# Sixth output pair and one tile of the seventh transposed on VectorE, the last tile on TensorE, rows of output pairs loaded two products sooner

## The chip, the core and the metric

The kernel runs on one core of a Trainium2 chip. The core has TensorE (PE in the profile; its weight loads are PEld), VectorE (DVE), ScalarE (ACT), GpSimd (POOL) and SyncE (SP). DMAs are issued from the queues of SP, ACT and POOL. The metric is the device time of one execution in microseconds; less is better. All data are fp32.

## What is computed

The reference, cut to what matters:

```python
def reference(x, adj, W_q, b_q, W_k, b_k, W_v, b_v):
    h = jnp.maximum(_layernorm(x, axis=-1), 0.0)            # x: 2708 x 1024
    q, k, v = h @ W_q.T + b_q, h @ W_k.T + b_k, h @ W_v.T + b_v
    z = (q @ k.T) / sqrt(1024) * adj                        # adj: 2708 x 2708, about 4 ones in a row
    z = jnp.where(z == 0.0, -10000.0, z)
    return x + jax.nn.relu(softmax(z, axis=1) @ v)
```

## The kernel before

**Algebra.** W_q and W_k are multiplied first, so that a query row is one product of h with a matrix M, and a score is the dot product of a query row with a gathered row of h. The softmax-weighted sum of gathered rows of h gives a tile u of 128 rows and 1024 columns, and u times W_v is the output before relu and the addition of x. Rows are sorted by their number of ones in adj, so that a tile needs as many gathers as its fullest row has ones. There are 22 tiles.

**Units.** TensorE works through 20 units, numbered from 0. Units 0 to 9 are query pairs. Units 10 to 19 are output pairs, of the tiles (6, 5), (4, 3), (2, 0), (20, 7), (17, 13), (18, 12), (19, 11), (15, 10), (14, 1) and (16, 9); the sixth output pair is thus unit 15, the seventh unit 16. Tile 8 stands alone behind them and is called the single tile. A pair is done by seven products of blocks instead of eight (`multiply`, L1045): `s2`, `a12`, `s4`, `s3` of the unit, then `a11` and `s1` of the next one (`opened`), then `a22` of the unit. Every product is four matmuls of 128x512 in the program (eight rows of the trace, since fp32 takes two passes), all in `add_block`, L1011. Between the products the function `after(i)`, i from 0 to 6, does the work of other engines for slot i.

**Turning.** A product needs its left operand transposed. There are two ways. TensorE turns a tile with eight 128x128 matmuls against an identity (`half_turned`, L415; the results `pt` lie in PSUM; ScalarE copies them out as `a11`, `a12`, `a22`, L718, or VectorE reads them in the sums `s1` and `s3`, L722). Or the tile is "faced": when its sum u is complete, ScalarE writes a permuted copy v (L945), v goes to `u_dram`, SP loads it in four quarters (`by_quarters`, L700), and VectorE transposes 32x32 blocks, two instructions of 128x512 per tile (`faces`, L705). The function `sums` decides which way a tile goes when it is complete (L940). A tile that is not faced is stored and loaded whole (L951, L1212), or, if its unit is near, kept in SBUF as `u` (`held`).

**Attention.** VectorE forms the scores (L863, one instruction per gathered 128x1024 block), the weights (L906 to L911), and the sums u (L923, one instruction per gathered block; the first block of a tile is scaled by ScalarE, L912). These steps are a generator that `after` advances by a fixed number of estimated microseconds per slot, less a little for faced tiles. The gathered blocks `g` are loaded by indirect DMAs that POOL issues (L610) into slots that VectorE's sums set free; query tiles `pq` come by SP (L833). L929 is the last sum of the single tile, half a tile high.

**Order.** VectorE's instructions stand in program order from unit 4 on; TensorE's, ScalarE's, POOL's and SP's are placed by the scheduler when the program is built. Each engine then runs its own list in order and waits on semaphores. Rows of output pairs (`or`) are loaded by `load_rows` in slot 4 two units ahead (slot 2 in units 4 and 9). Seven buffers hold rows, sums and permuted copies.

Of the kernel before, what the change touches and what calls it, by code (L numbers as in the profile page):

```python
# [10 lines left out]
FT = mybir.dt.float32  # L11
# [7 lines left out]
P = 128  # L19
# [46 lines left out]
def tile_preln_masked_attention(  # L66
# [13 lines left out]
    N, D = x.shape  # L80
    DC = D // P
# [336 lines left out]
    def turned(xt, name):  # L418

        hT = work.tile([P, D], FT, tag="hT", name=f"T_{name}", bufs=2).rearrange("p (c q) -> p c q", q=P)  # L420
        for s in range(DC // 4):
            nc.scalar.copy(hT[:, s * 4:(s + 1) * 4, :], half_turned(xt, s))
        return hT
# [190 lines left out]
    rows_of = {}  # L614
# [88 lines left out]
    def faces(dst, xt, lo, hi):  # L703

        return nc.vector.transpose(dst.rearrange("p c (g r) -> p g c r", r=QP),  # L705
                                   xt.rearrange("p (g c r) -> p g c r", g=QUADS, r=QP)[:, :, lo:hi])
# [212 lines left out]
    def sums(t):  # L919
        u, coef, m = us.pop(t)  # L920
        for s in range(0 if t in EMPTY else 1, K[t]):
            fill()
            chained(lambda: nc.vector.scalar_tensor_tensor(  # L923
                u, g_of[t][s], coef[:, s:s + 1], u, op0=ALU.mult, op1=ALU.add))
            free.append(g_of[t][s])
            yield 1.3
        fill()
        if t in HOSTS:
            chained(lambda: nc.vector.scalar_tensor_tensor(  # L929
                u[:HP], g_of[t][K[t]][:HP], m[:HP, 3:4], u[:HP], op0=ALU.mult, op1=ALU.add))  # L930
            free.append(g_of[t][K[t]])
            yield 1.3
            fill()
        g_of.pop(t)
        if t == SECOND:
            nc.sync.dma_start(v_dram, u)
            whole_second.append(True)
            return
        unit = next((n for n, pair in enumerate(units) if pair[0] == "o" and t in pair[1:]), len(units))
        if now < [unit - 2, 2] and unit <= len(q_pairs) + 4 or unit >= len(units) - 1:  # L940
            faced_tiles.add(t)
        print("done", t, "at", now, "unit", unit, t in faced_tiles)
        if t in faced_tiles:
            v = row_tile(f"v_{t}")
            nc.scalar.copy(v.rearrange("p (a c r) -> p c a r", a=QUADS, r=QP),  # L945
                           u.rearrange("p (c a r) -> p c a r", a=QUADS, r=QP))
            nc.scalar.dma_start(u_dram[t * P:(t + 1) * P, :], v)
        elif near(t):
            held[t] = u
        else:  # L950
            nc.sync.dma_start(u_dram[t * P:(t + 1) * P, :], u)  # L951
        done.add(t)
# [277 lines left out]
    for n, unit in enumerate(units):  # L1230
        kind, ta, tb = unit
        now[:] = n, 0
        if n == FIRST:
            ordered.close()
            ordered.enter_context(tc.manual_schedule(engines={mybir.EngineType.DVE}))
            nc.sync.dma_start(bp_dram, bp_sb[0:1, :])
        turn = n in (0, FIRST - 1)
        share = (20.9 if n < len(units) - 5 else 21.5) / 7
        nxt = units[n + 1] if n + 1 < len(units) else None
        if nxt is not None and nxt[0] == "o":  # L1240
            share -= 2.3 / 7 * len(set(nxt[1:]) & faced_tiles)
        results = (q_results if kind == "q" else o_results)(ta, tb)

        def after(i):
            now[1] = i
            add_due()
            if (n, i) in steps_ahead:
                follow(steps_ahead[n, i])
            if (n, i) == (2, 5):
                owe(8)  # L1250
                owe(9)
                rows_of[FIRST] = load_rows(units[FIRST])
                owe(10)
                owe(6)
                owe(7)
                rows_of[FIRST + 1] = load_rows(units[FIRST + 1])
                pooled.close()
            if n == FIRST and i in (1, 4, 5):
                for g in slots[:4] if i == 1 else slots[4:6] if i == 4 else slots[6:8]:
                    with tc.issue_after(sorted_at[-1].ins):  # L1260
                        nc.vector.memset(g, 0.0)
            b11, b12, b21, b22 = M[:, 0, 0], M[:, 0, 1], M[:, 1, 0], M[:, 1, 1]
            for at, place, src in (((-1, 0), b12, of_wv(0, 1)), ((0, 0), b11, of_wv(0, 0)), ((0, 2), T[:, 1], of_wv(1, 1)),
                                   ((0, 3), b21, of_wv(1, 0)), ((0, 4), b22, of_wv(1, 1))):
                if (n - last_q, i) == at:
                    nc.sync.dma_start(place, src)
            for at, place, a, b in (((0, 2), T[:, 0], b12, b11), ((0, 4), T[:, 1], T[:, 1], T[:, 0]),
                                    ((1, 0), T[:, 2], b22, b12), ((1, 1), T[:, 3], b21, T[:, 1])):
                if (n - last_q, i) == at:
                    nc.vector.tensor_sub(place, a, b)  # L1270
            if (n - last_q, i) == (1, 1):
                free.extend(M.rearrange("p i j (a c) w -> p i j a (c w)", a=2)[:, 0, 1, a, :] for a in range(2))
            if (n, i) == (FIRST, 5):
                next(stream)
            if (n, i) == (FIRST, 6):
                chain.append(behind[-1])
                next(stream)
                nc.vector.tensor_tensor(bad, bad, total, op=ALU.not_equal)
            if (n, i) == (FIRST + 1, 6):
                marked(EARLY, NT)  # L1280
            if (n, i) == (FIRST + 2, 4):
                nc.vector.tensor_scalar(msq, msq, MLIMIT, None, op0=ALU.is_gt)
            if n > FIRST + 1 or n == FIRST + 1 and i > 1:
                advance(share)
            if nxt is not None:

                if i == (3 if n == 0 else 4 if turn else 0):
                    ops_of[n + 1] = blocks(*rows_of[n + 1], nc.gpsimd if n + 1 < FIRST - 1 else None)
                    with tc.issue_after(products[-1].ins) if n + 1 == FIRST else nullcontext():
                        ops_of[n + 1][1]()  # L1290
                if i == (4 if n == 0 else 5 if turn else 2):
                    ops_of[n + 1][2]()
                    rows_of.pop(n + 1)
                    if n == last_q - 1:
                        all_rows()
                if i == 3:
                    banks_of[n + 1] = banks_for(bp_sb)
                if i == 6 and n + 2 < FIRST:
                    natural_rows(n + 2)
                if i == (2 if n in (FIRST, last_q) else 4) and n + 2 > FIRST and n + 2 < len(units) and n + 2 not in rows_of:  # L1300
                    while units[n + 2][0] == "o" and not done.issuperset(units[n + 2][1:]):
                        advance(1.0)
                    rows_of[n + 2] = load_rows(units[n + 2])
            if (n, i) in steps_at:
                follow(steps_at[n, i])
            if (n, i) == (3, 4):
                searched()
            if (n, i) == (3, 6):
                for s in range(8, HIGH):
                    for c in range(0, D, D // 4):  # L1310
                        with tc.issue_after(entered[-1].ins):
                            nc.gpsimd.memset(slots[s][:, c:c + D // 4], 0.0)
            if i == 3 and units[n - 1][0] == "o" and NT - 2 in units[n - 1][1:]:
                tail(NT - 1)
            if nxt is None and i == 1:
                uT = work.tile([P, D], FT, tag="hT", name="T_alone", bufs=2).rearrange("p (c q) -> p c q", q=P)
                faces(uT, single["rows"], 0, DC)
                single["turned"] = uT
            if n == len(units) - 2 and i == 6:
                while alone not in done:  # L1320
                    advance(1.0)
                single["rows"], = load_rows(("o", alone))
            if nxt is None and i == 3:
                single["banks"] = banks_for(bp_sb)
            if n == last_q - 1 and i == 4:

                nc.sync.dma_start(bp_sb, bv.to_broadcast([P, D]))
            if (n, i) == (last_q, 1):
                nc.vector.tensor_sub(bp_sb[:, NB:], bp_sb[:, NB:], bp_sb[:, :NB])

        multiply(n, results, after)
# [231 lines left out]
```

## Time and profile before

| what | us |
|---|---|
| median of 3 runs (lowest, highest) | 637.94 (637.57, 638.15) |
| the profiled execution | 638.0 |
| its span, from first to last instruction | 636.3 |
| TensorE busy in the span | 624.6 |
| VectorE busy | 525.7 |
| ScalarE busy | 283.5 |
| GpSimd busy | 361.8 |
| mean granted clock of TensorE | 0.995 |

In timelines the first number of a row is the start in us from the beginning of the span, the second the time until the last of the merged instructions ends, xN their count, and brackets hold the idle time of the engine before the row and who ended it. In the chain of waits the first number is the time, the second how long the chain stayed there.

### The profile page before, as it was taken

What the parts mean: (1) busy time and instruction counts of PE and PEld (TensorE: products, weight loads), DVE (VectorE), ACT (ScalarE), POOL (GpSimd) and SP (SyncE); (2) the same over time, 40 slices, a digit from 0 to 9 for tenths busy, and PEclk for the clock granted to TensorE, in tenths of its full rate; (3) what the DMA queues carried; (4) which work ended last, traced back from release to release, by engine and by line L of the source; (5) the groups of instructions that cost most, each with busy time, mean ns of one, the idle gap of its engine ahead of it and who ended that gap; (6) DMA issues with size and microseconds to landing.
All of it is one profiled execution on the core that took longest, in us unless ns stands there. A gap on an engine that the chain in (4) does not pass through costs nothing.

```text
span 636.3 us, 6139 instructions
## 1 busy us (share of the span) xinstructions
PE 624.6 (98%) x1627; PEld 315.5 (50%) x1627; DVE 525.7 (83%) x1021; ACT 283.5 (45%) x421; POOL 361.8 (57%) x383
## 2 busy tenths in 40 slices
PE   9999999999999999999999999999999999999994
PEld 5777766444444544444444434444444444444441
DVE  5999889897995755997889999999999989898341
ACT  3539975859667533424341243443343333422300
POOL 2649960975868277563742563576566777632431
PEclk9999999999999999999999999999999999999997
DMA  8998897598696439986699998999999999893761
GB/s 339 407 372 310 334 351 298 199 342 328 246 382 221 170 113 334 326 299 196 194 289 323 297 412 216 311 318 324 351 378 321 334 299 295 242 289 95 210 217 40
DMA packets 62352, 180.11 MB, mean 283 GB/s; under 512 B 10039, under 2 KB 17031, under 8 KB 61672
## 3 DMA queue, kind: packets, MB, share of 16 engines
q0 software_dynamic: 25136, 78.41, 39.4%
q1 hardware_dynamic: 31242, 80.19, 35.8%
q10 hardware_dynamic: 5934, 21.06, 8.5%
q8 instruction: 15, 0.25, 0.2%
q14 instruction: 25, 0.20, 0.1%
HBM read 147.23 MB, written 42.31 MB: 298 GB/s over the span
## 4 chain that ended last, share of the span: by engine, by line
PE 85%; DVE 6%; issue 4%; DMA 3%; SPq 1%; POOL 0%; ACT 0%; POOLq 0%; DVEq 0%; ACTq 0%
PE ps L1011 38%; PE psy L1011 28%; PE ps_y L476 6%; PE ps_x L476 4%; PE ps_z L476 4%; PE pt L415 3%; DVE u L923 2%; DMA g<-h_dram,tab 1%; DMA or<-u_dram 1%; DVE junk L863 1%; DVE s L722 1%; DVE wlow L1270 1%; PE ps_y L511 1%; SPq L700 1%; DVE q L1092 0%
## 5 line engine op out<-in xcount | busy, mean ns | idle before, releaser
L610 POOL DMA_INDIRECT g<-h_dram,tab x94 | 121.4, 1291 | 84.4 <-DVE u L923 31.1
L1011 PE MATMUL ps<-M,a 128*128 128x512 f32 x320 | 144.0, 593 | 0.0
L1011 PE MATMUL psy<-wlow,s 128*128 128x512 f32 x320 | 143.9, 592 | 0.0
L863 DVE SCALAR_TENSOR_TENSOR junk<-g,pq 128x1024 uint8<-128x1024 f32 x93 | 113.7, 1222 | 14.0 <-DMA g<-h_dram,tab 10.9
L1011 PEld LDWEIGHTS ps<-M,a 128*128 128x128 f32 x320 | 59.8, 190 | 70.8 <-issue 70.6
L1011 PEld LDWEIGHTS psy<-wlow,s 128*128 128x128 f32 x320 | 59.7, 190 | 70.2 <-issue 69.4
L923 DVE SCALAR_TENSOR_TENSOR u<-g,coef,u 128x1024 f32<-128x1024 f32 x69 | 88.4, 1281 | 6.9 <-ACT u L912 5.8
L389 DVE FIND_INDEX8 at<-ones,adj 128x8 uint32<-128x685 f32 (+1 forms) x88 | 74.5, 865 | 0.0
L1011 PE MATMUL psy<-wlow,a 128*128 128x512 f32 x160 | 72.0, 593 | 1.4 <-DVE q L1092 1.4
L1011 PE MATMUL ps<-M,s 128*128 128x512 f32 x160 | 72.1, 592 | 0.0
L1011 PE MATMUL ps<-wlow,s 128*128 128x512 f32 x160 | 72.0, 593 | 0.1
L368 ACT ACTIVATE sized<-adj 128x2708 uint8<-128x2708 f32 (+1 forms) x22 | 54.3, 2468 | 7.5 <-DMA adj<-in_adj_dram 6.2
L298 POOL TENSOR_TENSOR hsum<-hsum,x 128x256 f32<-128x256 f32 (+1 forms) x56 | 38.7, 729 | 25.6 <-DVE wlow L444 21.2
L1110 POOL DMA_INDIRECT y<-in_x_dram,tab x19 | 34.8, 1832 | 29.1 <-ACT y L1127 15.9
L1011 PEld LDWEIGHTS psy<-wlow,a 128*128 128x128 f32 x160 | 30.3, 190 | 40.0 <-issue 37.1
L1011 PEld LDWEIGHTS ps<-wlow,s 128*128 128x128 f32 x160 | 30.3, 190 | 38.6 <-issue 37.9
L1011 PEld LDWEIGHTS ps<-M,s 128*128 128x128 f32 x160 | 30.3, 190 | 38.1 <-issue 37.4
L912 ACT ACTIVATE u<-g,coef 128x1024 f32<-128x1024 f32 x18 | 20.7, 1147 | 32.1 <-DVE coef L911 32.1
L808 POOL DMA_INDIRECT out_dram<-y,tab x21 | 25.0, 1188 | 16.4 <-DVE flag L1354 6.1
L626 POOL DMA_INDIRECT tab_dram<-tab,pos_i x22 | 21.9, 995 | 20.7 <-DVE pos_i L689 15.3
L276 ACT ACTIVATE x<-x,r 128x1024 f32<-128x1024 f32 (+1 forms) x22 | 25.9, 1235 | 7.3 <-POOL r L266 7.3
L760 ACT COPY ps<-bp_sb 128x512 f32<-128x512 f32 x42 | 24.5, 595 | 7.2 <-DVE y L1145 6.7
(251 smaller groups left out, 843.5 us busy)
## 6 DMA issues: line engine op xcount, KB each, us to landing
adj<-in_adj_dram SPq DMA_DIRECT2D x21, 1354.0 KB, 11.3
x<-in_x_dram SPq DMA_DIRECT2D x21, 512.0 KB, 3.9
h_dram<-x ACTq DMA_DIRECT2D x21, 512.0 KB, 8.7
u_dram<-v ACTq DMA_DIRECT2D x13, 512.0 KB, 6.4
or<-u_dram SPq DMA_DIRECT2D x52, 128.0 KB, 7.0
q_late<-q SPq DMA_DIRECT2D x12, 512.0 KB, 6.0
pq<-q_late SPq DMA_DIRECT2D x12, 512.0 KB, 8.6
M<-in_wv_dram SPq DMA_DIRECT2D x4, 1024.0 KB
```

What stands on the lines that cost most here:

```text
L276: nc.scalar.activation(xs[i][:n], xs[i][:n], AF.Relu, bias=r[:n, 4, i:i + 1], scale=r[:n, 3, i:i + 1])
L298: small.append(nc.gpsimd.tensor_add(hsum[:n, cols], hsum[:n, cols], xt[:n, cols]))
L368: nc.scalar.activation(sized[:n], a[:n, :, :PW], AF.Abs, accum_out=total[:n, t:t + 1])
L389: nc.vector.max_index(at[:n, k - first_k, g, :], ones[:n, 0:8], a[:n, g, :])
L476: mm = nc.tensor.matmul(bank, a_tile(o + H * a[0], a[1], i), b(o), start=first and o == 0, stop=(o == H - 1), skip_group_check=True)
L610: return nc.gpsimd.indirect_dma_start(out=dst, out_offset=None, in_=src, in_offset=off, bounds_check=N - 1, oob_is_err=False)
L760: nc.scalar.copy(return_[h], row[:, h * NB:(h + 1) * NB])
L808: to = nc.gpsimd.indirect_dma_start(out=out, out_offset=bass.IndirectOffsetOnAxis(ap=ptab.bitcast(U32)[:n, t, SLOTS:SLOTS + 1], axis=0), i ...
L863: chained(lambda: nc.vector.scalar_tensor_tensor(junk, g_of[t][s], 1.0, tq[t], op0=ALU.mult, op1=ALU.mult, accum_out=zall[:, t, s:s + 1]))
L923: chained(lambda: nc.vector.scalar_tensor_tensor(u, g_of[t][s], coef[:, s:s + 1], u, op0=ALU.mult, op1=ALU.add))
L1011: mm = nc.tensor.matmul(bank, a[:, c, :], b[:, c, :], start=False, stop=(c == 3), skip_group_check=True)
L1110: return nc.gpsimd.indirect_dma_start(out=y[:n], out_offset=None, in_=x, in_offset=off, compute_op=ALU.add)
```

## The change

It has three parts. Tiles up to unit 16 may be faced, if they are complete by slot 0 two units ahead (before: up to unit 14, by slot 1). The single tile is no longer faced: it stays in SBUF, and TensorE turns it in slot 1 of the last unit. And rows of an output pair are loaded in slot 2 instead of 4 when both tiles are complete by then.

```diff
@@ sums
-        if now < [unit - 2, 2] and unit <= len(q_pairs) + 4 or unit >= len(units) - 1:
+        if now < [unit - 2, 1] and unit <= len(q_pairs) + 6 or unit == len(units) - 1:
             faced_tiles.add(t)
@@ after
-                if i == (2 if n in (FIRST, last_q) else 4) and n + 2 > FIRST and n + 2 < len(units) and n + 2 not in rows_of:
+                ready = n >= last_q and n + 2 < len(units) and done.issuperset(units[n + 2][1:])
+                if (i == 4 or i == 2 and (n == FIRST or ready)) and n + 2 > FIRST and n + 2 < len(units) and n + 2 not in rows_of:
                     while units[n + 2][0] == "o" and not done.issuperset(units[n + 2][1:]):
                         advance(1.0)
                     rows_of[n + 2] = load_rows(units[n + 2])
@@ after
             if nxt is None and i == 1:
-                uT = work.tile([P, D], FT, tag="hT", name="T_alone", bufs=2).rearrange("p (c q) -> p c q", q=P)
-                faces(uT, single["rows"], 0, DC)
-                single["turned"] = uT
-            if n == len(units) - 2 and i == 6:
                 while alone not in done:
                     advance(1.0)
-                single["rows"], = load_rows(("o", alone))
+                r, = load_rows(("o", alone))
+                single["turned"] = turned(r, "alone")
```

`turned` (L420) is the kernel's own function for one whole tile: two calls of `half_turned` and two copies by ScalarE (L422). In the changed program tiles 18, 12 and 19 are faced beside those that were before; tile 11, the other one of unit 16, is not.

The first place is TensorE's list where tile 18 was turned, at the seam of units 13 and 14. In the names `or_18` is the loaded tile 18, `u_11` a tile in SBUF, and the last number counts buffers. Before:

```order
L1011 MATMUL psy_2825<-wlow_171,a22_2740 128x512 x4
L415 MATMUL pt_2991<-ident_75,or_18_2928 128x128 x4
L415 MATMUL pt_2998<-ident_75,or_18_2928 128x128 x4
L1011 MATMUL psy_2950<-wlow_171,s2_2879 128x512 x4
L415 MATMUL pt_3027<-ident_75,or_12_2930 128x128 x4
L415 MATMUL pt_3034<-ident_75,or_12_2930 128x128 x4
L1011 MATMUL ps0_2908<-M_148,a12_2856 128x512 x4
```

In the change the same stretch has products alone, and VectorE has this instead, between sums of tile 11 and scores for tile 10:

```order
L923 TENSOR_SCALAR u_11_2939<-M_148,coef_2938,u_11_2939 128x1024
L705 STREAM_TRANSPOSE a11_3003<-or_18_2887 128x4x4x32
L705 STREAM_TRANSPOSE a12_3005<-or_18_2887 128x4x4x32
L923 TENSOR_SCALAR u_11_2939<-M_148,coef_2938,u_11_2939 128x1024
L863 TENSOR_SCALAR junk2_3010,zall_102<-g10_1413,pq_10_2975 128x1024
L863 TENSOR_SCALAR junk2_3018,zall_102<-g0_1403,pq_10_2975 128x1024
L705 STREAM_TRANSPOSE a22_3020<-or_12_2892 128x4x4x32
L705 STREAM_TRANSPOSE s3_3022<-or_12_2892 128x4x4x32
L722 TENSOR_TENSOR s1_3024<-a22_3020,s3_3022 128x512
L742 TENSOR_TENSOR s3_3022<-a11_3003,s3_3022 128x512
```

Two transposes come in per faced tile; the four sums that follow are as many as before.

The second place is VectorE's list around the sum that reads the product `s4` of unit 16 (L1126). Before, five of the six sums of tile 1 stood ahead of it (the last two of the five are shown here, and behind L1126 the sixth):

```order
L722 TENSOR_TENSOR s4_3373<-a12_3319,s2_3371 128x512
L923 TENSOR_SCALAR u_1_3302<-g0_1403,coef_3301,u_1_3302 128x1024
L923 TENSOR_SCALAR u_1_3302<-g1_1404,coef_3301,u_1_3302 128x1024
L1126 TENSOR_TENSOR u2_3331<-ps1_3230,u2_3331 128x512
L923 TENSOR_SCALAR u_1_3302<-g2_1405,coef_3301,u_1_3302 128x1024
L863 TENSOR_SCALAR junk2_3399,zall_102<-M_148,pq_9_3333 128x1024
```

In the change all six stand behind it:

```order
L1126 TENSOR_TENSOR u2_3299<-ps1_3201,u2_3299 128x512
L923 TENSOR_SCALAR u_1_3332<-g8_1411,coef_3331,u_1_3332 128x1024
L923 TENSOR_SCALAR u_1_3332<-g9_1412,coef_3331,u_1_3332 128x1024
L923 TENSOR_SCALAR u_1_3332<-g10_1413,coef_3331,u_1_3332 128x1024
L923 TENSOR_SCALAR u_1_3332<-g0_1403,coef_3331,u_1_3332 128x1024
L923 TENSOR_SCALAR u_1_3332<-g1_1404,coef_3331,u_1_3332 128x1024
L923 TENSOR_SCALAR u_1_3332<-g2_1405,coef_3331,u_1_3332 128x1024
L863 TENSOR_SCALAR junk2_3382,zall_102<-M_148,pq_9_3351 128x1024
```

Five sums moved to the later side of a step that depends on TensorE.

The third place is TensorE's list at the start of the last unit. Before:

```order
L1011 MATMUL ps1_3657<-wlow_171,s1_3641 128x512 x4
L1011 MATMUL psy_3588<-wlow_171,a22_3519 128x512 x4
L1011 MATMUL psy_3685<-wlow_171,s2_3644 128x512 x4
L1011 MATMUL ps0_3655<-M_148,a12_3613 128x512 x4
L1011 MATMUL ps1_3657<-M_148,s4_3646 128x512 x4
```

In the change:

```order
L1011 MATMUL ps1_3640<-wlow_171,s1_3624 128x512 x4
L1011 MATMUL psy_3571<-wlow_171,a22_3502 128x512 x4
L415 MATMUL pt_3686<-ident_75,u_8_3604 128x128 x4
L415 MATMUL pt_3692<-ident_75,u_8_3604 128x128 x4
L1011 MATMUL psy_3665<-wlow_171,s2_3627 128x512 x4
L1011 MATMUL ps0_3638<-M_148,a12_3596 128x512 x4
```

The turning of the single tile, `u_8`, now stands ahead of the product `s2` of the last unit, and everything that TensorE has left stands behind it. It reads the tile whose last sum is VectorE's L929.

## The prediction

> **What bounds the kernel now.** I read the page's busy times first, then the chain of waits, the waits of TensorE, the stages of the output pairs, and last the timelines of the two engines that the change moves work between.
>
> ```profile
> span 636.3 us, 6139 instructions
> PE 624.6 (98%) x1627; PEld 315.5 (50%) x1627; DVE 525.7 (83%) x1021; ACT 283.5 (45%) x421; POOL 361.8 (57%) x383
> PE psy L1011 <- DVE q L1092: 1.4, 1, 1.4
> PE ps_y L511 <- POOL hsum L121: 1.2, 1, 1.2
> 368.16 0.61 DVE q L1092
> 368.81 7.13 PE psy L1011 x16
> 546.30 0.87 PE pt L415 x8
> 627.28 0.70 DVE y_alone L1379
> ```
>
> The third and fourth rows are all that TensorE waited for in the whole span: 1.4 and 1.2. The last four are from the chain of waits: from 368.81 the chain stays on TensorE until VectorE's last sum at 627.28. So nothing after 368.81 waits for anything but TensorE's own list. A group of turning, the eight transposes of one tile, lies on this chain with 0.87. (In the timeline below such a group has 1.04, since its last row ends after the next product has begun.)
>
> ```profile
> 471.00:497.00 26.00, 26.00 (x74) 12.43 (x73) 23.71 (x41) 9.77 (x18) 18.36 (x15) 1.00 1.01 323
> 522.00:548.00 26.00, 26.00 (x74) 12.42 (x73) 23.79 (x34) 10.08 (x19) 17.00 (x13) 1.00 0.91 288
> ```
>
> These are two stages of about one unit each (stretch, its length, then busy time with count of PE, PEld, DVE, ACT, POOL; last the clock, DMA share, GB/s). TensorE is full at clock 1.00, but VectorE is busy for 23.71 and 23.79 of 26: it has little more than 2 us of air per unit. The work goes from the engine that bounds to one that nearly does.
>
> **What TensorE saves.** Before, it turns the tiles of units 15 to 18: 18, 12, 19, 11, 15, 10, 14 and 1, eight groups. Now 11, 15, 10, 14, 1 and the single tile: six. Saved 2 x 0.87 = 1.74, if TensorE stays without a pause.
>
> **Where a pause can come.** The single tile's group is put ahead of `s2` of the last unit and reads u_8, whose last sum is VectorE's L929.
>
> ```profile
> 546.14 1.04 PE L415 MATMUL pt<-ident,u 128*128 128x128 f32 x8
> 592.52 3.60 PE L1011 MATMUL psy<-wlow,a 128*128 128x512 f32 x8
> 595.95 3.60 PE L1011 MATMUL psy<-wlow,s 128*128 128x512 f32 x8
> 620.21 7.03 PE L1011 MATMUL ps<-M,T_alone 128*128 128x512 f32 x16
> 591.14 1.27 DVE L929 SCALAR_TENSOR_TENSOR u<-g,m,u 64x1024 f32<-64x1024 f32 x1
> ```
>
> TensorE comes to that place at 595.95 now, and its last matmul ends at 620.21 + 7.03 = 627.24. With five groups instead of eight ahead of it, it gets there 3 x 0.87 = 2.61 earlier, at 593.34. From there it has 0.87 + (627.24 - 595.95) = 32.16 to do. Hence its new end is the later of 593.34 and the time at which u_8 is ready, plus 32.16. Behind the last matmul stay the same 9.06 us of the span and 1.7 around it (638.0 - 636.3).
>
> Before, u_8 is ready at 591.14 + 1.27 = 592.41, 0.93 ahead of 593.34. So VectorE may become late by 0.93 for nothing; every us beyond is paid in full, and behind the waiting group stand all products of the last unit and of the single tile. At a delay of 0.93 + 1.74 = 2.67 the saving is gone.
>
> **What VectorE takes on.** Six transposes of 128x512, two for each of 18, 12, 19. The four sums per tile that follow remain, only with SBUF for PSUM as a source in two of them.
>
> ```profile
> 573.69 1.30 DVE L705 STREAM_TRANSPOSE a<-or 128x512 f32<-128x512 f32 x2
> 574.92 0.12 DVE L906 SCALAR_TENSOR_TENSOR w<-w,keys 128x8 f32<-128x8 f32 x1
> 476.19 1.28 DVE L722 TENSOR_TENSOR s<-a,pt 128x512 f32<-128x512 f32 x2 [1.04 <-ACT a L718]
> 480.77 1.23 DVE L863 SCALAR_TENSOR_TENSOR junk<-g,pq 128x1024 uint8<-128x1024 f32 x1 [0.82 <-DMA g<-h_dram,tab]
> 500.99 1.23 DVE L863 SCALAR_TENSOR_TENSOR junk<-g,pq 128x1024 uint8<-128x1024 f32 x1 [0.96 <-DMA g<-h_dram,tab]
> 510.87 0.69 DVE L1122 TENSOR_TENSOR p<-taken,p 128x512 f32<-128x512 f32 x1 [0.28 <-ACT taken L1076]
> 523.78 1.22 DVE L863 SCALAR_TENSOR_TENSOR junk<-M,pq 128x1024 uint8<-128x1024 f32 x1 [1.83 <-DMA M<-h_dram,tab]
> 551.48 2.61 DVE L923 SCALAR_TENSOR_TENSOR u<-g,coef,u 128x1024 f32<-128x1024 f32 x2 [1.62 <-ACT u L912]
> 564.34 0.69 DVE L1122 TENSOR_TENSOR p<-taken,p 128x512 f32<-128x512 f32 x1 [0.95 <-ACT taken L1076]
> 576.93 3.92 DVE L923 SCALAR_TENSOR_TENSOR u<-g,coef,u 128x1024 f32<-128x1024 f32 x3 [1.22 <-ACT u L912]
> ```
>
> Two transposes take 574.92 - 573.69 = 1.23, so six take 3.7. Against that stand idle times, in brackets with who ended them. The wait for `a` L718 (1.04) goes, because ScalarE's eviction of turned tiles of unit 15 goes; the waits for `taken` (0.28, 0.95) are waits for a TensorE that will now be earlier against VectorE. Sum 2.27; 3.7 - 2.27 = 1.43 if the waits for gathered blocks (0.82, 0.96, 1.83) neither grow nor shrink. They can do both: a late VectorE finds blocks landed, but it also frees their slots late.
>
> The 3.7 cannot simply be spread, though, since the order moved. Tile 1's five sums now stand behind L1126 of unit 16, which must wait for a product:
>
> ```profile
> 528.97 3.60 PE L1011 MATMUL ps<-M,s 128*128 128x512 f32 x8
> 533.81 0.69 DVE L1126 TENSOR_TENSOR u<-ps,u 128x512 f32<-128x512 f32 x1
> 493.47 6.56 DVE L923 SCALAR_TENSOR_TENSOR u<-g,coef,u 128x1024 f32<-128x1024 f32 x5
> ```
>
> That product ends at 528.97 + 3.60 = 532.57; with three groups fewer ahead (18, 12, 19) at 532.57 - 2.61 = 529.96. From L1126 to L929 VectorE has 591.14 - 533.81 = 57.33 now, plus five sums (6.56 by the row of five), less the 0.95 for `taken`: 62.94. The earliest L929 is 529.96 + 62.94 = 592.90, u_8 is ready at 594.17, 1.76 late; TensorE pauses 594.17 - 593.34 = 0.83, and 1.74 - 0.83 = 0.91 would be left. This is a floor: VectorE has no way to be ahead of it, unless one of its other waits in the stretch closes (1.62 and 1.22 for the first block that ScalarE scales; nothing of that is removed). I add one wait for a gathered block of the usual kind, 0.82, since VectorE now frees five slots of tile 1 later and POOL reloads them for the next tiles. The delay is then 2.58, u_8 ready at 594.99, the pause 1.65, and 594.99 + 32.16 = 627.15 against 627.24: a gain of 0.09.
>
> A rule bears on the transposes: the Trainium skill, page "VectorE: DVE Perf Modes", section "Rules for kernel authors", gives 128x128 transposes to TensorE where PSUM will do, and 32x32 ones to VectorE. The rows have 0.87 per tile on the one and 1.23 on the other, which agrees with its ranking; if the rule alone decided here, the change would lose as rival B does.
>
> **Edits costed at nothing, and their cover.** Three permuted copies v come in and one goes:
>
> ```profile
> 592.44 1.05 ACT L945 COPY v<-u 128x1024 f32<-128x1024 f32 x1 [0.55 <-DVE u L929]
> 388.11 4.82 SPq L700 DMA_DIRECT2D or<-u_dram  x8
> 403.11 1.30 DVE L705 STREAM_TRANSPOSE a<-or 128x512 f32<-128x512 f32 x2
> pq<-q_late SPq DMA_DIRECT2D x12, 512.0 KB, 8.6
> or<-u_dram SPq DMA_DIRECT2D x36, 128.0 KB, 6.9
> ```
>
> Each copy is 1.05 on ScalarE, which is 45% busy and loses the evictions of three turned tiles; uncovered it is 2 x 1.05 = 2.1 in all. Quarter loads of a tile take four issues on SP instead of one. Eight took 4.82 and were all issued by 392.93; with the median of 6.9 to landing that is 399.8, 3.3 ahead of their first use at 403.11. For a faced tile these are three issues more than before, 3 x 4.82 / 8 = 1.8; a query tile queued behind them on SP starts that much later, and if it is late already, VectorE's scores wait as much more: part of rival C. Loading rows in slot 2 asks for a free one of the seven buffers, and where there is none the issue only waits longer: I give it no gain and, because SP's other issues then stand behind it, no more than that same loss.
>
> The single tile's store, quarter loads and 128x1024 transpose go, and with them this wait:
>
> ```profile
> 605.03 1.25 DVE L705 STREAM_TRANSPOSE T_alone<-or 128x1024 f32<-128x1024 f32 x1 [11.56 <-DMA or<-u_dram]
> 609.69 3.60 PE L1011 MATMUL ps<-M,T_alone 128*128 128x512 f32 x8
> ```
>
> It ends at 606.28, and TensorE wants T_alone only at 609.69; so the 11.56 cost nothing before, and their removal gains nothing. In the changed order ScalarE copies T_alone out of PSUM behind the turning near 594, over 10 us ahead of that product.
>
> **The rivals.** *A: VectorE comes in time.* For it: its idle times for gathers sum to 3.6 and would cover all 3.7 if the blocks came no later. Against it: L1126 sets a floor 0.83 too late. The end would be 593.34 + 32.16 = 625.50, that is 638.0 - 1.74 = 636.3; it needs a delay of at most 0.93.
>
> *B: all six transposes reach L929*, because the waits that vanish come back elsewhere. For it: VectorE has only 2.3 of 26 us idle in a stage. Against: two of the vanishing waits are waits for TensorE, which really is earlier. u_8 ready at 592.41 + 3.7 = 596.11, the end 628.27, 1.03 more: 639.0.
>
> *C, slower: the late VectorE also waits for its gathers.* The slots that POOL fills are freed by L923, the sums that slip; query tiles stand behind more issues on SP. For it: DMA share at 1.01 and 0.91 in the stages above, and the longest wait, 1.83, is of this kind. Against: a late engine needs its blocks later too. One such wait on top of B: a delay of 3.7 + 1.83 = 5.53, the end 592.41 + 5.53 + 32.16 = 630.10, 2.86 more: 640.9. It decides from a delay of 2.67 + 1.28 = 3.95.
>
> That the change does not do what it says can hold only for the early loads, which move no term.
>
> **How the numbers follow.** A measurement of this kernel can tell some 0.2%, 1.28 us, from no change. Forecast 638.0 - 0.09 = 637.9, chance 0.53, for delays from the floor's 1.76 to 3.3, that is 637.1 to 638.6. A: 0.13. B: 0.16. C: 0.18. Faster by over 0.2% needs a delay of at most 1.39: A and 0.02 of the forecast, 0.15. Slower by over 0.2%: C and 0.05 of B, 0.23. The rest, 0.62, is within. The range goes from just below A, 636.1, up to B and a part of C, 639.9; the forecast's own stands above. I take the forecast and not the floor itself, because the floor supposes that no wait of VectorE grows over 63 us.
>
> **What would show it.** Six groups of turning, the last one near 593.3, with idle time of 0.8 to 2 ahead of it in TensorE's timeline and VectorE's L929 as releaser; from there 32.2 to TensorE's end. L929 starts between 592.9 and 594.5. VectorE idles ahead of L1126 of unit 16, with TensorE's `ps` as releaser. No pause there would be A; one over 3, with bracketed waits for `g` or `pq` ahead of scores from 500 on, would be C. Wrong in another way would be a pause of TensorE ahead of units 15 or 16, where the faced tiles came too late: then the pause that counts is not the one I priced.

## The result and the profile after

| | kernel before | changed kernel |
|---|---|---|
| median, us (runs) | 637.98 (6) | 642.93 (6) |
| lowest to highest | 637.57 to 638.51 | 638.22 to 645.19 |
| the profiled execution, us | 638.0 | 638.22 |
| its span | 636.3 | 636.4 |
| TensorE busy | 624.6 | 623.1 |
| VectorE busy | 525.7 | 528.7 |

The ratio is 1.007, with a 95% interval from 1.005 to 1.0091: the change made the kernel slower by 5 us, and its time spreads over 7 us where it had spread over 1. Forecast were 637.9 and no measurable change; the median lies above the range.

The profiled execution is the fastest of the six, and it looks as forecast. TensorE's waits, its rows around the single tile's turning, VectorE's L929 ahead of it, and TensorE's last row:

```profile
PE pt L415 <- DVE u L929: 1.4, 1, 1.4
PE ps L1011 <- DVE s L722: 0.6, 1, 0.6
```
```profile
590.19 3.60 PE L1011 MATMUL psy<-wlow,a 128*128 128x512 f32 x8
595.18 1.06 PE L415 MATMUL pt<-ident,u 128*128 128x128 f32 x8 [1.40 <-DVE u L929]
596.08 3.60 PE L1011 MATMUL psy<-wlow,s 128*128 128x512 f32 x8
...
620.34 7.03 PE L1011 MATMUL ps<-M,T_alone 128*128 128x512 f32 x16
```
```profile
476.00 1.23 DVE L863 SCALAR_TENSOR_TENSOR junk<-g,pq 128x1024 uint8<-128x1024 f32 x1 [3.73 <-DMA pq<-q_late]
...
593.76 1.27 DVE L929 SCALAR_TENSOR_TENSOR u<-g,m,u 64x1024 f32<-64x1024 f32 x1
```

u_8 is ready at 595.03 (forecast 594.99), the pause is 1.40 (1.65), TensorE ends at 627.37 (627.15). But the delay does not come from where it was put. Before L1126 of unit 16 VectorE has no idle time; it lost 3.73 at 476 waiting for a query tile, that of tile 10. SP's timeline (a row is an issue or several, not a transfer) has it as the second of two in the kernel before:

```profile
443.62 8.91 SPq L833 DMA_DIRECT2D pq<-q_late  x2
...
460.85 0.80 SPq L1212 DMA_DIRECT2D or<-u_dram  x2
```

In the changed kernel the eight quarter loads of tiles 18 and 12 stand ahead of it:

```profile
443.12 13.37 SPq L700 DMA_DIRECT2D or<-u_dram  x8
459.49 0.34 SPq L833 DMA_DIRECT2D pq<-q_late  x1
```

Whole, the two tiles took SP 0.80; in quarters they hold it for 13.37. The query tile is issued at 459.49 instead of about 452.2 (443.62 + 8.91 less one issue). Most of this is waiting. SP's waits from 441 to 459.6 in the changed kernel (us in total, times, longest):

```profile
SPq L700 <- DMA or<-u_dram: 6.1, 4, 2.7
SPq L700 <- DMA u_dram<-v: 4.7, 1, 4.7
SPq L833 <- DMA or<-u_dram: 2.9, 1, 2.9
SPq L700 <- DMA pq<-q_late: 2.4, 1, 2.4
```

That is 9.0 for the landing of earlier pieces, 4.7 for the store of the second tile's copy v and 2.4 for an earlier query tile. Behind the waits for pieces is a detail of the trace: SP's transfers take turns at eight semaphores, and an issue waits until the transfer that used its semaphore last has landed. The query tile at 459.49 waits for the piece issued at 444.78, which took 14.6 to land. A tile in four pieces uses four of the eight turns instead of one.

Then the query tile takes longer to land. The issues by form, for 440 to 480 of the kernel before and 455 to 480 of the changed one (last number: median us to landing):

```profile
pq<-q_late SPq DMA_DIRECT2D x3, 512.0 KB, 9.4
```
```profile
pq<-q_late SPq DMA_DIRECT2D x2, 512.0 KB, 16.4
```

459.49 + 16.4 is the 476 at which VectorE goes on. The 9.4 is that of the query tile issued at 464.56, since the profile has no landing for the one at 452.2; the others that it has in the kernel before behind 400 are 8.6 and 5.7. Over the whole span, the waits of quarter loads for the landing of earlier pieces went from 0.2 to 11.8 (kernel before, then changed kernel):

```profile
SPq L700 <- DMA or<-u_dram: 0.2, 1, 0.2
```
```profile
SPq L700 <- DMA or<-u_dram: 11.8, 7, 2.7
```

One execution that ends well is no account of a median 4.7 us above it, so the rest comes from experiments.

### The profile page after: what moved, and what is told of

It is laid out like the page before. It is cut to its first block, busy times and chain, and to the rows that moved or that the text cites. A ratio compares the mean times of both kernels' runs of the same rounds, so it can differ in the third digit from the quotient of the medians.

```text
span 636.4 us, 6110 instructions
## 1 busy us (share of the span) xinstructions
PE 623.1 (98%) x1611; PEld 313.7 (49%) x1611; DVE 528.7 (83%) x1026; ACT 283.5 (45%) x420; POOL 360.6 (57%) x383
## 4 chain that ended last, share of the span: by engine, by line
PE 81%; DMA 7%; DVE 5%; POOL 3%; ACT 2%; issue 1%; ACTq 0%; POOLq 0%; SPq 0%; DVEq 0%
PE ps L1011 36%; PE psy L1011 26%; PE ps_y L476 6%; PE ps_x L476 4%; PE ps_z L476 4%; PE pt L415 3%; POOL hsum L298 2%; DMA x<-in_x_dram 2%; DMA q_late<-q 2%; DVE u L923 1%; DMA u_dram<-v 1%; DVE s L722 1%; DMA M<-in_wv_dram 1%; DMA wlow<-in_wk_dram 1%; ACT sized L368 1%
## 5 line engine op out<-in xcount | busy, mean ns | idle before, releaser
L610 POOL DMA_INDIRECT g<-h_dram,tab x94 | 119.8, 1274 | 76.3 <-DVE u L923 30.4
L808 POOL DMA_INDIRECT out_dram<-y,tab x21 | 25.9, 1232 | 16.0 <-DMA y<-in_x_dram,tab 7.1
L945 ACT COPY v<-u 128x1024 f32<-128x1024 f32 x15 | 15.7, 1046 | 32.9 <-DVE u L923 30.4
```

The costliest lines, as they stand in the source:

```text
L610: return nc.gpsimd.indirect_dma_start(out=dst, out_offset=None, in_=src, in_offset=off, bounds_check=N - 1, oob_is_err=False)
L808: to = nc.gpsimd.indirect_dma_start(out=out, out_offset=bass.IndirectOffsetOnAxis(ap=ptab.bitcast(U32)[:n, t, SLOTS:SLOTS + 1], axis=0), i ...
```

## The experiments

Each of the four groups ran on one chip beside the kernel before, whose median there was 641.44, 640.08, 638.13 and 638.12. Ratios are to the kernel before in the same group; they are not the quotients of the medians shown. They are compared across groups, times are not.

| run | what it is | median, us | ratio, 95% interval |
|---|---|---|---|
| e1 | the change again | 646.18 | 1.0061, 1.0037 to 1.0084 |
| e2 | without the earlier loads | 646.32 | 1.0064, 1.0035 to 1.0094 |
| e3 | single tile turned later | 643.16 | 1.0020, 0.9991 to 1.0049 |
| e4 | facing alone | 646.79 | 1.0073, 1.0042 to 1.0104 |
| e5 | kernel before, one run | 639.06 | |
| e6 | facing, no v, whole loads | 638.18 | 0.9965, 0.9951 to 0.9978 |
| e7 | single tile alone | 640.63 | 1.0012, 0.9997 to 1.0026 |
| e8 | earlier loads alone | 640.45 | 1.0009, 0.9992 to 1.0026 |
| e9 | facing, v, whole loads | 636.98 | 0.9993, 0.9973 to 1.0012 |
| e10 | facing, no v, quarter loads | 642.63 | 1.0077, 1.0060 to 1.0094 |
| e11 | facing, permuted stores for all | 642.33 | 1.0072, 1.0058 to 1.0086 |
| e12 | e3 with permuted stores for all | 642.70 | 1.0093, 1.0071 to 1.0114 |
| e13 | facing, permuted stores for three | 644.76 | 1.0102, 1.0084 to 1.0120 |
| e14 | the change, permuted stores for three | 637.16 | 0.9988, 0.9972 to 1.0005 |
| e15 | facing, permuted stores for five | 637.24 | 0.9987, 0.9974 to 1.0000 |
| e16 | e14 and e3 | 636.96 | 0.9975, 0.9964 to 0.9986 |

### The change again, and one part undone

e1 is the change unedited.

> The changed kernel once more, unchanged. Its six times so far lie between 638.2 and 645.2, and the one that was profiled was the fastest of them (638.2, a pause of 1.4 us of TensorE at the single tile's turning). All theories expect a median of 641 to 644 and a spread of several us. If this profile comes from a slower execution (span over 639), theory Q (query tiles land late: they stand behind the quarter loads of faced tiles in SP's queue) expects VectorE idle ahead of scores with a load of pq as releaser, 3 us more in sum than in the first profile, and a pause of TensorE at the single tile's turning longer by as much. Theory F (the rows of a faced tile land late) expects pauses of TensorE in units 14 to 16 instead, ended by VectorE's transposes or sums of tiles 18, 12 or 19. Theory S (the three added tiles are simply too much work for VectorE) expects the same busy time, no idle time on VectorE from 500 on, and does not explain the spread.

Its profile fell on its slowest execution, span 648.9. TensorE's rows with a pause, and the one behind the last:

```profile
374.12 5.40 PE L1011 MATMUL psy<-wlow,a 128*128 128x512 f32 x8 [3.89 <-DVE q L1092]
500.43 3.70 PE L1011 MATMUL psy<-wlow,s 128*128 128x512 f32 x8 [0.68 <-ACT psy L1024]
587.98 3.70 PE L1011 MATMUL psy<-wlow,s 128*128 128x512 f32 x8 [0.50 <-ACT u L1055]
596.44 3.67 PE L1011 MATMUL ps<-wlow,s 128*128 128x512 f32 x8 [1.33 <-DVE s L722]
...
605.98 1.06 PE L415 MATMUL pt<-ident,u 128*128 128x128 f32 x8 [2.44 <-DVE u L929]
606.88 5.29 PE L1011 MATMUL psy<-wlow,s 128*128 128x512 f32 x8
...
632.84 7.03 PE L1011 MATMUL ps<-M,T_alone 128*128 128x512 f32 x16
```

The first row is the seam between query and output pairs, at 368.55 in the first profile; 5.57 of this execution's excess lies ahead of it, where TensorE, VectorE and SP have the same instructions in both kernels, so we do not count it to the change. From that row's start to TensorE's end are 639.87 - 374.12 = 265.75, against 258.82 in the first profile and 627.24 - 368.81 = 258.43 before. Of the 6.93 more, 2.93 are pauses (0.68 + 0.50 + 1.33 + 2.44 against 1.40 + 0.62), and 3.39 are two products that take 5.40 and 5.29 instead of 3.70 and 3.60; 0.6 is in smaller gaps. VectorE again waits 3.40 for a query tile, and then 2.76 and 2.58 for gathered blocks. The new thing is how lateness reaches TensorE at 500. ScalarE's rows there, and VectorE's L1122, whose sum L1123 reads:

```profile
499.16 0.63 ACT L1123 ACTIVATE y<-p 128x512 f32<-128x512 f32 x1 [5.50 <-issue]
499.70 0.19 ACT L872 ACTIVATE w<-zall 128x6 f32<-128x6 f32 x1
499.79 0.58 ACT L1024 COPY psy<-ps 128x512 f32<-128x512 f32 x1
```
```profile
493.69 0.69 DVE L1122 TENSOR_TENSOR p<-taken,p 128x512 f32<-128x512 f32 x1
```

Behind L1123 in ScalarE's order stands the copy L1024, which TensorE needs at 500.43. VectorE's sum was complete at 494.38, so it is not what held L1123 until 499.16. POOL's rows, first in the kernel before, then in e1:

```profile
465.54 1.64 POOL L1110 DMA_INDIRECT y<-in_x_dram,tab  x1 [1.42 <-DMA tail_dram<-y]
```
```profile
481.52 1.56 POOL L1110 DMA_INDIRECT y<-in_x_dram,tab  x1 [10.53 <-DMA tail_dram<-y]
490.74 2.08 POOL L808 DMA_INDIRECT out_dram<-y,tab  x1 [0.30 <-issue]
```

`tail_dram<-y` is a transfer of 4 KB that SP issues among its loads (at 460.53 before, at 468.49 in e1). POOL went on 5.0 after that issue before and 13.0 after it in e1, and the output transfer L808 followed late. ScalarE's L1123 waits for transfers, and most likely for this one: the profile names no releaser in e1, but in the first profile of the change the same wait ends at 490.75, when the output transfer issued at 481.58 has landed after 9.1. So here lateness went, as far as the rows show, from SP's transfers by POOL and ScalarE to TensorE, and not by VectorE's sum. At 587.98 it went by VectorE:

```profile
587.24 0.21 ACT L872 ACTIVATE w<-zall 128x8 f32<-128x8 f32 x1 [6.52 <-DVE junk L863]
587.36 0.57 ACT L1055 COPY u<-psy 128x512 f32<-128x512 f32 x1
```

L872 waits for VectorE's scores, and the copy L1055 behind it is the one that TensorE needs. TensorE is thus stopped before the single tile too.

e2 puts the loads back into slot 4; e3 moves the single tile's turning; e4 is the kernel before with only the rule for facing changed:

```diff
e2
-                ready = n >= last_q and n + 2 < len(units) and done.issuperset(units[n + 2][1:])
-                if (i == 4 or i == 2 and (n == FIRST or ready)) and n + 2 > FIRST and ...
+                if i == (2 if n in (FIRST, last_q) else 4) and n + 2 > FIRST and ...
e3
-            if nxt is None and i == 1:
+            if nxt is None and i == 3:
                 while alone not in done:
e4, against the kernel before
-        if now < [unit - 2, 2] and unit <= len(q_pairs) + 4 or unit >= len(units) - 1:
+        if now < [unit - 2, 1] and unit <= len(q_pairs) + 6 or unit >= len(units) - 1:
```

> The change without its third part: rows of output pairs are loaded in slot 4 as before; the facing of tiles 18, 12, 19 and the single tile on TensorE stay. If the loads put ahead of the query tiles delay these (theory Q), the time falls to 637 to 639 with a spread under 1 us, and the idle time for pq falls below 1 us. If the rows of faced tiles come late anyway (theory F), it gets slower than the change, 643 to 648, since the rows are loaded later. If it is VectorE's work (theory S), it stays at 641 to 644.

> The change with the single tile's turning two products later on TensorE (slot 3 instead of slot 1 of the last unit); VectorE's and SP's work before it is the same. If the whole loss is the pause ahead of that turning (theories Q and S), up to 6.9 us of delay of u_8 are now hidden, and the time falls to 636.3 to 638, with a small spread. If TensorE pauses earlier, in units 14 to 16 or at the sums s1 of the last unit (theory F), most of the loss stays: 640 or more.

> The kernel before with tiles 18, 12 and 19 faced, rows loaded as before, and the single tile faced as before. TensorE has five groups of turning instead of eight, 2.61 us less. u_8 is 1.8 to 2.6 us later, and T_alone, ready at 606.3 before, comes at 608 to 609 against a need at 607.1: theory S gives 636.5 to 638. Theory Q expects the same here, with a small spread. Theory F expects 640 or more, with pauses of TensorE in units 14 to 16.

e2 is no faster than e1, so the earlier loads are not the cause; its VectorE waits for the rows themselves:

```profile
477.80 1.30 DVE L705 STREAM_TRANSPOSE a<-or 128x512 f32<-128x512 f32 x2 [5.72 <-DMA or<-u_dram]
...
485.47 0.71 DVE L705 STREAM_TRANSPOSE a<-or 128x512 f32<-128x512 f32 x1 [2.74 <-DMA or<-u_dram]
```

Where the pieces go first, the query tile is late; where the query tiles go first, the pieces are. e3 takes the pause at the single tile away and some 3 us of the loss with it, but 1.47, 0.86 and 1.33 of other pauses remain, and the 1.74 of two groups do not appear: that wait was one of the places, not the cause. In e4 nothing is left of the change but the facing, and it is as slow; there the late u_8 reaches TensorE through T_alone:

```profile
620.24 5.40 PE L1011 MATMUL ps<-M,T_alone 128*128 128x512 f32 x8 [3.15 <-DVE T_alone L705]
```

None of the three theories had said this whole. Q (query tiles late behind the quarter loads) had the right queue and expected e2 to be fast; F (rows late) expected the times of e3 and e4, but e4's pause is not in units 14 to 16; S (VectorE's work alone) and Q had e4 at 636.5 to 638.

### VectorE's work, or the way of the tile

e5 is the kernel before. e6 keeps e4's transposes, but stores and loads tiles 18, 12 and 19 as the kernel before did:

```diff
-        if t in faced_tiles:
+        if t in faced_tiles and t not in (18, 12, 19):
             v = row_tile(f"v_{t}")
...
+                if t in (18, 12, 19):
+                    faced.append(rows[-1])
-                if t in faced_tiles:
+                if t in faced_tiles and t not in (18, 12, 19):
                     by_quarters(rows[-1], u_dram[t * P:(t + 1) * P, :])
```

(A tile still held in SBUF is marked in the same way.) e6 and, below, e9 and e10 leave out a part of the permutation, so blocks of these three tiles lie in wrong places; only the times of these kernels are of use. e7 and e8 put the other two parts of the change, as its diff has them, into the kernel before.

> The kernel before, unchanged, for a profile beside the next ones. Where its time is above 639, theory V (VectorE's reserve: executions differ in when blocks, rows and query tiles land, and the kernel before still absorbs it in the output pairs) expects the excess ahead of the seam at about 369 us, where both kernels have the same instructions, and pauses of TensorE after it below 1 us in sum. Theory N (the executions after the change were disturbed, the change is not at fault) expects pauses behind the seam here as well, 2 us or more.

> The kernel with the facing alone (e4), but tiles 18, 12 and 19 are stored and loaded whole and unpermuted, as in the kernel before; VectorE still makes the same six transposes of them, so that the output of these tiles is left wrong and the work stays. It has VectorE's added 3.7 us and TensorE's saved 2.6 us without the copies v and without the quarter loads. Theory W (the added work alone uses up VectorE's reserve): as slow as e4, 4 to 6 us over the kernel before on the same chip. Theory D (the detour of a faced tile, by v, store and quarter loads in SP's queue, is late and VectorE, in order, waits for rows or query tiles): 1 to 2.6 us faster than the kernel before, with waits of VectorE for rows and query tiles under 1 us in sum behind 460.

> The kernel before with the single tile's part of the change alone: not faced, kept in SBUF, turned by TensorE in slot 1 of the last unit. Units 15 and 16 and the loads of rows stay as before. TensorE has one group more: 0.87 us slower than the kernel before if u_8 comes in time, as it does by 3.5 us in the profile of before. Theory V: 0.5 to 1.5 us slower, no pause of TensorE at that turning. If the wait for u_8 is at fault by itself: 3 us slower or more.

> The kernel before with the earlier loading of rows alone (slot 2 instead of 4 where both tiles are complete). Theory D: the loads go ahead of query tiles in SP's queue; VectorE waits up to 1 us more for these, TensorE saves and loses nothing: within 1 us of the kernel before. If the earlier loads were the cause: 3 us slower or more.

e5 reaches the seam at 369.67 and ends TensorE at 628.30: 258.63 from there, as in the first profile of before, with 0.3 of pauses. One execution at 639 does not show what the kernel before does in its slowest ones. e6 is faster than the kernel before by 0.35%, 2.2 us of the 2.61 that three groups less are worth on TensorE: **all of VectorE's added work fits**. e7 and e8 are harmless, 0.1% each. In e8 VectorE waits 3.83 for a query tile at 449.77, as long as in the change, and TensorE has no pause behind 393: without the added transposes VectorE has the reserve for it. What is left of the facing is the tile's way: the copy v, its store, and the quarter loads.

### Copy or quarter loads

e9 keeps v and loads whole; e10 keeps the quarter loads and stores u without v.

```diff
e9, against e4
-                    by_quarters(rows[-1], u_dram[t * P:(t + 1) * P, :])
+                    if t in (18, 12, 19):
+                        faced.append(rows[-1])
+                        nc.sync.dma_start(rows[-1], u_dram[t * P:(t + 1) * P, :])
+                    else:
+                        by_quarters(rows[-1], u_dram[t * P:(t + 1) * P, :])
e10, against e4
-        if t in faced_tiles:
+        if t in faced_tiles and t not in (18, 12, 19):
             v = row_tile(f"v_{t}")
```

> The facing alone (e4) with the copies v and their stores kept, but tiles 18, 12 and 19 loaded whole, with one issue on SP in place of four quarter loads; their blocks then stand in the wrong places and these output rows are left wrong, the work of every engine stays. Theory D1 (the quarter loads: they stand long in SP's queue, and rows and query tiles are late): 1 to 2.6 us faster than the kernel before, waits of VectorE for rows and query tiles under 1.5 us in sum behind 460. Theory D2 (the copy v: it waits in ScalarE's order, and the store starts later than the one on SP did): still 4 to 6 us slower than the kernel before.

> The facing alone (e4) with the quarter loads kept, but tiles 18, 12 and 19 stored as they are by SP, as in the kernel before, with no copy v; their blocks are not permuted inside, so these output rows are left wrong. Theory D1: as slow as e4, 4 to 6 us over the kernel before, with waits of VectorE for rows or query tiles of 3 us or more in sum behind 460. Theory D2: 1 to 2.6 us faster than the kernel before. Between the two, both have a share.

With quarter loads, 1.0073 (e4) and 1.0077 (e10); with whole loads, 0.9965 (e6) and 0.9993 (e9), with v or without. **The quarter loads are it.** VectorE's waits for rows and query tiles behind 369, without the single tile's, say the same: 4.8 (e4) and 4.7 (e10) against 1.2 (e6) and 1.2 (e9), although e10's profile fell on its fastest execution. What v costs is not settled: 0.28% between e6 and e9, whose intervals just overlap, and nothing between e4 and e10. e9 gains less than the 1 to 2.6 us that were expected of it.

### The permutation moved to the store

e11 and e12 store v in four pieces of 32 rows to the places that the loaded tile wants, for every faced tile, and load it whole:

```diff
-            nc.scalar.dma_start(u_dram[t * P:(t + 1) * P, :], v)
+            to = u_dram[t * P:(t + 1) * P, :].rearrange("(a r) (g j) -> g r a j", a=QUADS, g=QUADS)
+            for g in range(QUADS):
+                nc.scalar.dma_start(to[g], v[g * QP:(g + 1) * QP, :].rearrange("r (a j) -> r a j", a=QUADS))
```

> The facing alone (e4), for all faced tiles with the permutation moved from the load to the store: ScalarE's queue stores v in four pieces of 32 rows into the places where the loaded tile wants them, and SP loads it whole with one issue. It computes the same. If the pieces hurt only because query tiles and rows stand behind them in SP's queue: 1 to 2.6 us faster than the kernel before. If pieces of 1 KB are slow on whichever queue, the store lands later by as much as the load is shorter: 0 to 5 us slower than the kernel before, with the same waits of VectorE for rows.

> The change with the single tile's turning in slot 3 (e3) and the permuted stores with whole loads of e11. TensorE has two groups fewer than the kernel before, 1.74 us. If the detour of the faced tiles was all that was wrong: 0.5 to 1.7 us faster than the kernel before, pauses of TensorE behind 369 below 1 us in sum. If not: as e3, 0 to 3 us slower.

Both are slow, e12 by more than the 3 us that were allowed for, but elsewhere. Behind 403 TensorE has no pause left in either profile. ScalarE's queue and TensorE in e11:

```profile
372.48 1.77 ACTq L946 DMA_DIRECT2D u_dram<-v  x3
```
```profile
392.44 3.70 PE L1010 MATMUL ps<-wlow,s 128*128 128x512 f32 x8 [2.81 <-DVE s L719]
402.89 6.49 PE L1010 MATMUL psy<-wlow,s 128*128 128x512 f32 x8 [3.32 <-ACT psy L1023]
```

Now the pieces stand in ScalarE's queue, at a place where VectorE (it waits 2.04 and 1.68 for ScalarE at 374 and 380) and TensorE soon need its copies. So the four last kernels do it only for later tiles: for 18, 12 and 19, or for 17 and 13 as well (e15, whose first store in pieces is at 407.28).

```diff
-            nc.scalar.dma_start(u_dram[t * P:(t + 1) * P, :], v)
+            if t in (18, 12, 19):
+                ...
+            else:
+                nc.scalar.dma_start(u_dram[t * P:(t + 1) * P, :], v)
...
+                    if t in (18, 12, 19):
+                        faced.append(rows[-1])
+                        nc.sync.dma_start(rows[-1], u_dram[t * P:(t + 1) * P, :])
```

e13 and e15 are e4 with this, e15 for 17 and 13 too; e14 is the change with this; e16 is e3 with this.

> The facing alone (e4) with permuted stores and whole loads for tiles 18, 12 and 19 only; the tiles of earlier units keep the quarter loads. It computes the same. If the queue of SP was the cause: 1 to 2.6 us faster than the kernel before, as e6, and no pauses at 382 to 403 beyond those of the kernel before. If pieces on ScalarE's queue hurt here too: 2 us slower or more, with TensorE ended by ScalarE's copies at 424 to 500.

> The change as it was, with permuted stores and whole loads for tiles 18, 12 and 19 and nothing else. If the quarter loads were all that the prediction missed, its sum holds here: 0.1 to 0.9 us faster than the kernel before, with one pause of TensorE of 0.8 to 1.7 us at the single tile's turning. If VectorE is late for another reason: 2 us slower or more, the pause 2.4 us or longer and a slow product behind it.

> As e13, with tiles 17 and 13 stored and loaded in the same way too. Eight quarter loads fewer stand in SP's queue: as e13 or up to 1 us faster where rows and query tiles still came late; slower than e13 if the stores in ScalarE's queue at about 424 delay its copies for TensorE.

> As e14 with the single tile's turning in slot 3. TensorE has two groups fewer than the kernel before and no pause at the single tile: 1.2 to 1.7 us faster than the kernel before, and 0.8 to 1.7 us faster than e14.

In e14 SP's loads of 18, 12 and 19 are single issues, the query tile of tile 10 is issued at 453.04, and the forecast's picture stands there, down to the idle time ahead of L1126 (L1131 in this file) of unit 16:

```profile
453.04 0.32 SPq L833 DMA_DIRECT2D pq<-q_late  x1
```
```profile
530.79 0.69 DVE L1131 TENSOR_TENSOR u<-ps,u 128x512 f32<-128x512 f32 x1 [1.08 <-PE ps L1016]
...
593.59 1.27 DVE L929 SCALAR_TENSOR_TENSOR u<-g,m,u 64x1024 f32<-64x1024 f32 x1
```
```profile
595.01 1.06 PE L415 MATMUL pt<-ident,u 128*128 128x128 f32 x8 [0.71 <-DVE u L929]
```

VectorE waits 0.4 in all for query tiles. e14's median is 0.96 below the kernel before, and its interval includes no change; e16's is 1.16 below, and its interval excludes no change: it beats both kernels. The four pieces per tile are still there, as stores on ScalarE's queue. From the seam (369.07) to TensorE's end (618.99 + 7.03) it takes 256.95, 1.48 less than before, with one pause of 0.33: together 1.8, the 1.74 of two groups.

e13 missed. The scheduler put three query tiles on SP ahead of the eight quarter loads of the tiles 17 and 13, which kept them; in the kernel before and in e4 there are two. SP, VectorE and TensorE there:

```profile
414.87 21.37 SPq L833 DMA_DIRECT2D pq<-q_late  x3
436.34 12.79 SPq L700 DMA_DIRECT2D or<-u_dram  x8
```
```profile
450.90 1.31 DVE L705 STREAM_TRANSPOSE a<-or 128x512 f32<-128x512 f32 x2 [4.67 <-DMA or<-u_dram]
```
```profile
469.72 5.40 PE L1016 MATMUL psy<-wlow,a 128*128 128x512 f32 x8 [4.64 <-ACT taken L1081]
```

In the kernel before the same eight start at 430.49 and take 7.86. In e13 SP waits 19.2 in these rows for VectorE's scores to free the buffers of query tiles, and then for stores of v, so the rows come late from the start; e13 therefore does not test the quarter loads of 18, 12 and 19 alone. e15, which takes the eight pieces of 17 and 13 off too, is back at 0.9987, 7.5 us below e13 where at most 1 had been expected.

## Why the prediction was wrong

**What TensorE saves: right.** e6 and e16 give most of the 2.61 and 1.74 back.

**Where a pause can come: right, and incomplete.** The place and the 32.16 behind it hold in the first profile (32.19) and in e14 (32.18). That "every us beyond is paid in full" is too little: behind longer pauses a product took 5.3 to 6.7 instead of 3.6. And it is not the only place: ScalarE's order hands the lateness of VectorE, and of transfers that POOL and SP issue, to TensorE at the seams too (e1, e3).

**What VectorE takes on: right.** The 3.7 fit, as e6, e14 and e16 show. The floor at L1126 is seen in e14, with u_8 ready at 594.86 (594.17 to 594.99 forecast); in the change itself the delay came from the query tile instead.

**"Edits costed at nothing, and their cover": this step failed.** It took three further quarter loads per tile for 1.8 us of issuing, 3.6 for the two tiles ahead of the query tile, and took their landing at the median of 6.9. It is not the issuing that was too low. The same view of the kernel before has two more rows of eight:

```profile
402.48 13.08 SPq L700 DMA_DIRECT2D or<-u_dram  x8
430.49 7.86 SPq L700 DMA_DIRECT2D or<-u_dram  x8
```

Of the first, one wait for the store of a copy v takes 9.0 (SP's waits from 402 to 416):

```profile
SPq L700 <- DMA u_dram<-v: 9.0, 1, 9.0
```

Of the second, two waits take 4.2. Without them both are shorter than 4.82. What the price left out are the waits between the issues, for stores of v and for the landing of earlier pieces; and the 6.9 hides that pieces of these two rows took up to 15.1 (402 to 440; four landings are known, 6.9 to 15.1). In the changed kernel the query tile was issued 7.3 later, not 3.6, and landed 16.4 after that, where 5.7 to 9.4 are known before. VectorE, whose sums were already at the edge, waited 3.73 for it. The quarter loads without v (e10) cost 0.77%, against a gain of 0.35% with neither quarter loads nor v (e6).

**The rivals.** C named what happened, a late VectorE that waits for query tiles behind more issues on SP; it got a chance of 0.18 and 640.9. Its price lacked the slow products and the way by POOL and ScalarE; measured were 4.95. e14, the change with the fault taken out, lies between the forecast's own gain of 0.09 and A's 1.74.

**One execution as the kernel.** The working stood against an execution of a kernel that spread over 1 us. The single execution that its sum describes is the lowest of the changed kernel's six. That the change took the reserve which made the time so steady is our reading, borne out by e8 but not varied by itself. What makes the pieces land sooner in one execution and later in another stays open: DMA share was near 1 in these stages in both kernels, but no run varied it, nor did one separate the small runs of a piece from the number of transfers under way. Nor does a profile show the median execution of the change.

## What to carry to other kernels

Price a moved transfer by what its queue may wait for between the issues, and not by the issues alone. Follow what stands behind it on its queue and who waits for that, ahead of counting engine work; here 3.7 us of work were free and twelve small loads cost 5. When a bound engine is full to the end, ask which reserve keeps its neighbours' noise away from it: here the loss showed in the spread, and not in the fastest execution. Where a layout must change on the way through memory, put the small pieces on the queue and at the time where nothing waits behind them.

## What the hardware showed

After some pauses of TensorE the next product took longer than its usual 3.60 to 3.70. Behind pauses up to 1.5 us it was no slower (1.47, then 3.70 in e3). From 1.9 to 2.9 it went both ways: 1.92 then 5.40 (e6), 1.90 then 3.70 (e10); 2.81 then 3.70 (e11), 2.81 then 6.69 (e12). All pauses from 3.1 on were followed by a slow one: 3.15 by 5.40 (e4), 3.32 by 6.49 (e11), 4.64 by 5.40 (e13). The granted clock goes with it: over the slow products it was 0.68 (5.40 in e4, e6 and e13) or 0.55 to 0.57 (6.69 in e12, 6.49 in e11), and 1.00 over the 3.70 of e10 and e11. The extra is 1.7 in most and 2.7 to 3.0 in three (e11, e12, and the seam of e4 with 6.41 behind a pause of 3.89).

The Trainium skill's page "TensorE: Matmul & The Clock Gate", section "What's actually happening", has the clock fall to half after an idle window of about 3.4 us, until a busy window of that length. By its figure the loss is estimated at half of 3.4, the 1.7 seen in most cases; the 2.7 to 3.0 are more than that. That pauses of 1.92 and 2.44 were enough goes against the length that it gives for the idle window.
